# Fourteen kept steps in place of seven: an attention kernel that transposes more of its exponentials instead of computing them twice

## The chip, the cores and the metric

The kernel runs on one core of a Trainium2 chip. Its engines work side by side and meet through semaphores: TensorE (PE in the profile; its weight loads are PEld), VectorE (DVE), ScalarE (ACT), GpSimd (POOL) and SyncE (SP), which here only issues DMA transfers. The metric is device time in microseconds of one execution; the median of 3 runs of the kernel before is 692.13 us (692.12 to 693.17).

## What is computed

A conditioned self-attention with a residual: 8 batches, 512 positions, width 512, 16 heads of 32.

```python
Q = _split_heads(x @ Wq.T + bq)
K = _split_heads(x @ Wk.T + bk)
V = _split_heads(x @ Wv.T + bv)
tQ = _split_heads(tokens @ Wq.T + bq)      # tokens: one row per batch
tK = _split_heads(tokens @ Wk.T + bk)
cQ = Q + tQ
cK = K + tK
scores = jnp.einsum('bhqd,bhkd->bhqk', cQ, cK) / jnp.sqrt(jnp.float32(HEAD_DIM))
attn = jax.nn.softmax(scores, axis=-1)
out = jnp.einsum('bhqk,bhkd->bhqd', attn, V)
return x + out.transpose(0, 2, 1, 3).reshape(B, S, D_MODEL)
```

All arithmetic is in 32-bit floats.

## The kernel before

**Steps.** The work is cut into T = 32 steps: step t is batch t // 4 and a group of four heads, which fill the 128 partitions with 4 x 32 rows. For a step the kernel needs three things: the row maxima and row sums of the scores (queries on the partitions), the exponentials with the keys on the partitions, and those times V.

**Two kinds of step.** In a *plain* step the scores are computed twice. First row by row (`row_scores`, L585): VectorE takes the negated maxima (`one_max`, `row_max_of`, L552 and L594), ScalarE takes exponentials whose only use is their sum (`denominators`, L640). The maxima are split into three bf16 parts (`split_max`), turned by a DMA transpose (`turn_max`, L666), and in the next step `exponentials` computes the scores again with keys on the partitions (L695), subtracts the maxima through a small matmul with ones (L692), and ScalarE writes the exponentials `e` (L706). In a *blocked* step the row exponentials of L640 are kept instead, in a buffer `blocks` of 128 x 8192 values, and turned: VectorE transposes every 32 x 32 square in place (`turn_blocks`, L605, eight units of 128 x 1024, unit n belonging to query chunk n // 2), and DMA transfers exchange squares between the four groups of 32 partitions. Before, the exchange (`swap_blocks`, L624) is a swap through two `between` buffers: for each half of the queries three moves of six transfers of 32 rows x 4 KB, each move after the one before. Such a step has no second scores, no `e` and no `maxT`. Blocked are the steps 3, 7, ... 27. There is one `blocks` buffer (pool `eb`, `bufs=1`).

**Items.** The loop over t = 1 ... 28 has four items a step: V (the weighted sum of step t - 1, `weighted`, and its output), and q, k, v, which project for a later batch. In each item TensorE does, in order, the second scores of t (plain steps), the row scores of step t + 1, query chunk i + 1 (in the last item: t + 2, chunk 0), and a product or the V sum. The projections use seven half-size products in place of eight for a 2 x 2 split (`MADE_OF`, products 1 to 7 of `product`, L441): the item of an odd step does products 1, 6, 7 and half of 2 (`first_products`, or `first_by_others` in blocked steps, where ScalarE copies and GpSimd adds), that of an even step 4, 5, 3 and the other half of 2 (`other_products`, whose adds are VectorE's).

**What sets the order.** TensorE, VectorE, ScalarE and GpSimd run what they are given in the written order (`manual_schedule`), and so, all but a few transfers at the start, does SyncE. PSUM has eight banks; `begin` and `released` hand them from item to item, so that an item's scores go to the banks that were freed first. `turn_more` says after which item how many units are turned, `SWAPS` after which item which move is issued; loads of x blocks and residuals are issued in the last item of a step, outputs at once in `send`.

## Time and profile before

| | |
|---|---|
| median of 3 runs | 692.13 us |
| span of the profiled execution (the page gives no other time of it) | 687.9 us |
| PE busy | 677.3 us (98%) |
| DVE busy | 563.3 us (82%) |
| ACT busy | 563.7 us (82%) |
| POOL busy | 233.3 us (34%) |
| granted TensorE clock | 1.000 |
| transfers of the exchange (L624) | 252 of 128 KB, 2.4 us from issue to landing |

A line of a timeline reads: start in us from the span's start, duration, engine, line of the kernel, operation, output<-input, and how many stand in it; in brackets the idle time ahead of it and what ended it. A line of the chain of waits has start, duration and the work that the end of the run is followed back through. Groups have the number of instructions, their busy time, the mean in ns and the idle time ahead. `SPq` are the DMA issues of SyncE; their duration is the issue, not the transfer. Instructions of one engine overlap a little at their ends, so the distance between two starts is the better measure of what one costs. A waiting matmul often shows no idle time: its weights' load is what waits, so the distance between items is again the better measure.

### The profile page before, as it was taken

Reading aid. Unit: us, or ns where it says so; the run is one execution under the profiler, and the core shown is the slowest. Engines: PE = TensorE matmul, PEld = TensorE weight load, DVE = VectorE, ACT = ScalarE, POOL = GpSimd, SP = SyncE. Lnnn points to the kernel's source line nnn. Section 1 sums busy time; section 2 is a strip of 40 time slices with the busy share of each in tenths; the row PEclk is TensorE's granted clock in tenths of the full one; section 3 lists DMA queues with packets and bytes.
Section 4 is the critical chain, followed back from the end, with each engine's and each line's share of the span. In section 5 each row is a group of like instructions: output and inputs, shape, how many; then the busy total and the mean of one; then the engine's idle time right before and its main releaser. Section 6 shows DMA issues by size and latency. Waiting matters only on the chain.

```text
span 687.9 us, 22054 instructions
## 1 busy us (share of the span) xinstructions
PE 677.3 (98%) x8824; PEld 311.7 (45%) x8824; DVE 563.3 (82%) x878; ACT 563.7 (82%) x1427; POOL 233.3 (34%) x315
## 2 busy tenths in 40 slices
PE   9999999999999999999999999999999999999997
PEld 7444444444445444444444444453544544444332
DVE  4798799967989689886998778996798967987777
ACT  2589887988879898898888988798887989888664
POOL 3722412424233242424314252252423324241361
PEclk9999999999999999999999999999999999999999
DMA  6633235654376543663456624665427622376311
GB/s 183 104 54 60 40 64 133 129 106 70 52 155 143 90 71 78 132 155 61 68 118 122 143 49 77 135 125 113 72 40 154 148 54 41 66 135 151 53 31 31
DMA packets 231674, 65.50 MB, mean 95 GB/s; under 512 B 221834, under 2 KB 222346, under 8 KB 231572
## 3 DMA queue, kind: packets, MB, share of 16 engines
q1 hardware_dynamic: 229812, 63.05, 47.4%
q8 instruction: 69, 1.13, 0.7%
q10 hardware_dynamic: 1760, 1.05, 0.5%
q14 instruction: 33, 0.27, 0.1%
HBM read 19.75 MB, written 8.39 MB: 41 GB/s over the span
## 4 chain that ended last, share of the span: by engine, by line
PE 88%; DMA 3%; POOL 3%; SPq 2%; ACT 1%; DVE 1%; issue 1%; DVEq 0%; POOLq 0%; ACTq 0%
PE psum L441 37%; PE psum L715 16%; PE psum L585 16%; PE psum L695 11%; PE psum L692 4%; PE psum L384 2%; DMA maxT<-split 2%; SPq L784 1%; ACT psum L640 1%; SPq L188 1%; DMA xr<-in_x_dram 1%; POOL res L781 1%; DMA w_q<-in_L_cond_Wq_dram 1%; DVE nmax L552 1%; PE psum L725 1%
## 5 line engine op out<-in xcount | busy, mean ns | idle before, releaser
L640 ACT ACTIVATE psum<-psum,nmax 128x512 f32<-128x512 f32 x368 | 244.7, 673 | 29.0 <-DVE nmax L552 21.2
L552 DVE TENSOR_REDUCE nmax<-psum 128x1 f32<-128x512 f32 x298 | 191.3, 683 | 79.6 <-PE psum L585 77.2
L706 ACT ACTIVATE e<-psum 128x512 f32<-128x512 f32 x376 | 194.2, 602 | 61.2 <-PE psum L695 57.7
L585 PE MATMUL psum<-kT,qT 32*128 32x512 f32 x1024 | 143.0, 605 | 0.0
L594 DVE TENSOR_REDUCE nmax<-psum 128x2 f32<-128x1024 f32 x101 | 122.5, 1214 | 1.3 <-PE psum L585 1.3
L695 PE MATMUL psum<-qT,kT 32*128 32x512 f32 x752 | 96.7, 587 | 0.0
L715 PE MATMUL psum<-e,v 128*32 128x512 f32 x800 | 95.3, 597 | 0.0
L780 POOL TENSOR_TENSOR res<-res,recs 128x512 f32<-128x512 f32 x30 | 31.4, 1048 | 172.4 <-DVE res L779 172.4
L196 POOL TENSOR_TENSOR xr<-xr,bvs 128x512 f32<-128x512 f32 x30 | 38.4, 1280 | 141.8 <-DMA xr<-in_x_dram 141.8
L585 PEld LDWEIGHTS psum<-kT,qT 32*128 32x128 f32 x1024 | 60.9, 182 | 52.7 <-issue 22.0
L640 ACT ACTIVATION_READ_ACCUMULATOR psum<-psum,nmax 128x1 f32 x368 | 78.7, 214 | 0.0
L640 ACT ACTIVATE blocks<-psum,nmax 128x512 f32<-128x512 f32 x112 | 76.2, 719 | 0.0
L605 DVE STREAM_TRANSPOSE blocks<-blocks 128x1024 f32<-128x1024 f32 x56 | 68.5, 1223 | 0.0
L441 PE MATMUL psum<-wc_v,xc 128*32 128x256 f32 x768 | 50.2, 379 | 0.0
L441 PE MATMUL psum<-xc,wc_q 128*32 128x256 f32 x720 | 47.1, 379 | 0.0
L441 PE MATMUL psum<-xc,wc_k 128*32 128x256 f32 x720 | 47.1, 379 | 0.0
L715 PEld LDWEIGHTS psum<-e,v 128*32 128x32 f32 x800 | 20.8, 110 | 51.4 <-issue 29.2
L692 PE MATMUL psum<-maxT,onesb 3*128 3x512 bf16 x376 | 37.1, 385 | 3.0 <-DMA maxT<-split 2.3
L781 POOL TENSOR_TENSOR res<-res,xr 128x512 f32<-128x512 f32 x30 | 38.5, 1282 | 2.4
L695 PEld LDWEIGHTS psum<-qT,kT 32*128 32x128 f32 x752 | 37.4, 185 | 1.7
L441 PE MATMUL psum<-wT_v,xT 128*32 128x256 f32 x512 | 36.8, 382 | 0.0
L779 DVE STREAM_TRANSPOSE res<-psum 128x512 f32<-128x512 f32 x28 | 20.1, 717 | 18.4 <-PE psum L715 15.4
(179 smaller groups left out, 862.9 us busy)
## 6 DMA issues: line engine op xcount, KB each, us to landing
between<-blocks SPq DMA_DIRECT2D x84, 128.0 KB, 2.4
blocks<-blocks SPq DMA_DIRECT2D x84, 128.0 KB, 2.3
blocks<-between SPq DMA_DIRECT2D x84, 128.0 KB, 2.4
out_dram<-res SPq DMA_DIRECT2D x122, 64.0 KB, 1.9
xr<-in_x_dram SPq DMA_DIRECT2D x120, 64.0 KB, 2.4
x<-in_x_dram SPq DMA_DIRECT2D x112, 64.0 KB, 2.4
w_q<-in_L_cond_Wq_dram SPq DMA_DIRECT2D x4, 256.0 KB, 4.2
w_v<-in_L_cond_Wv_dram SPq DMA_DIRECT2D x16, 64.0 KB, 2.3
```

What stands on the lines that cost most here:

```text
L196: nc.gpsimd.tensor_tensor(xr[t], xr[t], bias, ALU.add)
L441: nc.tensor.matmul(pt[r], still[:, r], moving, start=(kc == kcs[0]), stop=(kc == kcs[-1]))
L552: nc.vector.tensor_reduce(nmax[t][:, qc, j : j + 1, 0], pt, AX.X, ALU.max, negate=True)
L585: nc.tensor.matmul(pt, qkT["q", t][r, qc * P : (qc + 1) * P], qkT["k", t][r, :], start=True, stop=True,)
L594: nc.vector.tensor_reduce(nmax[t][:, qc, pr * 2 : pr * 2 + 2, 0], pt, AX.X, ALU.max, negate=True)
L605: nc.vector.transpose(e, e)
L640: nc.scalar.activation(to, of, AF.Exp, bias=nmax[t][:, qc, j, :], accum_out=sums[t][:, qc, j, :],)
L692: nc.tensor.matmul(bank[j], onesb[r, :], maxT[t][r, :], start=True, stop=False)
L695: nc.tensor.matmul(bank[j], qkT["k", t][r, kc * P : (kc + 1) * P], qkT["q", t][r, :], start=False, stop=True,)
L706: nc.scalar.activation(e[:, i, :], bank[pr * 2 + i], AF.Exp)
L715: nc.tensor.matmul(pt[j * HD : (j + 1) * HD, :], vs[b % 2][:, kc, (g * HG + j) * HD : (g * HG + j + 1) * HD], e, start=(kc == chunks[0]), ...
L781: nc.gpsimd.tensor_tensor(y, y, xr.pop(t), ALU.add)
```

## The change

The odd steps 1, 3, ... 27 are blocked, 14 instead of 7, and

- the row exponentials of a blocked step go to an `arena` of 14 rooms of 128 x 1024 (`rows_kept`: rooms 0 to 3 for the first half of the queries, 4 to 7 for the second); the `e` of plain steps use rooms 8 to 13, 0 and 1 (`room_for_e`). The pool of ten `e` buffers is gone;
- the exchange comes first and the turn after it: `exchange` moves each half with 16 transfers of 32 rows x 4 KB from the arena into `blocks`, none of which waits for another; then VectorE turns the eight units in place, one after each of the items k and v of the even step ahead, one after V and q of the odd step, two after k and v;
- in odd steps the items do products 1, 6, 2, 7 whole (`four_products`: ScalarE's copies, GpSimd's adds), in even steps 5, 4, 3 (`three_products`: VectorE's adds);
- the V item is always first; SyncE's work is listed by item (`ORDERS`): even steps issue the first exchange after V, and store, residual and the second exchange after k; odd steps store after q, residual and x blocks after k. `send` only puts its output on a list that `store` empties;
- x blocks have two buffers instead of three, `q`/`k` pairs two instead of three, residuals one; the turned maxima go into the unused half of `wT_v`; the residual's bias is added on GpSimd at the head of `weighted`.

```diff
@@ -68,14 +68,15 @@
-    BLOCKED = [t for t in range(3, T - 4, G)]
+    ROOMS = 14
+    BLOCKED = list(range(1, T - 4, 2))
...
-    xp = ctx.enter_context(tc.tile_pool(name="xp", bufs=3))
+    xp = ctx.enter_context(tc.tile_pool(name="xp", bufs=2))
...
-    qkp = ctx.enter_context(tc.tile_pool(name="qkp", bufs=3))
-    ep = ctx.enter_context(tc.tile_pool(name="ep", bufs=10))
+    qkp = ctx.enter_context(tc.tile_pool(name="qkp", bufs=2))
+    ep = ctx.enter_context(tc.tile_pool(name="ep", bufs=1))
@@ -181,19 +182,40 @@
-                xr[t] = late[0][:, 2, :].rearrange("p (f e) -> p f e", e=BL)
+                xr[t] = late_part(t % 2 * 10 + 2).rearrange("p (f e) -> p f e", e=BL)
...
-                xr[t] = op.tile([P, NB, BL], F32, tag="xr", name=f"xr_{t}")
+                xr[t] = op.tile([P, NB, BL], F32, tag="xr", name=f"xr_{t}", bufs=1)
...
-            bias = bvs[:, g, :].unsqueeze(1).broadcast_to([P, NB, BL])
...
+    def add_bias(t):
+        if turned_by_vector(t):
+            bias = bvs[:, t % G, :].unsqueeze(1).broadcast_to([P, NB, BL])
+        else:
...
+    arena = ep.tile([P, ROOMS, NP * S], F32, tag="arena", name="arena")
+    place = [0]
+    def room_for_e(t, kc, pr):
+        if t + 1 in BLOCKED and kc == 0 and pr == 0:
+            place[0] = 8
+        i = place[0]
+        place[0] = (i + 1) % ROOMS
+        return arena[:, i, :].rearrange("p (i s) -> p i s", s=S)
+    def rows_kept(t, half):
+        a = arena[:, half * HG : (half + 1) * HG, :]
+        return a.rearrange("p g (c h s) -> p g c h s", c=2, h=HG)
@@ -486,29 +508,43 @@
-    def first_by_others(n, b, u, dens, small, at):
+    def four_products(n, b, u, dens, small, at):
...
+        m1 = c2[:, 0, :]
...
+        product(n, b, u, 2, two_[:, :HS])
...
+            nc.scalar.copy(c1, two_.rearrange("p (h s) -> p h s", h=2) if c1.shape[1] == 2 else two_)
...
+            i = "qk".index(n)
+            nc.scalar.activation(c1, halves(two_), AF.Identity, bias=tok[:, i, u * 2, b : b + 1])
+            nc.scalar.activation(c22, one_[:, HS:], AF.Identity, bias=apart_tok[:, i, u, b : b + 1])
+        nc.gpsimd.tensor_tensor(c1, c1, twice(m1), ALU.add)
...
+    def three_products(n, b, u, dens, small, at):
+        dens()
+        one_, two_ = banks(at[0]), banks(at[1])
+        product(n, b, u, 5, one_[:, HS:])
+        product(n, b, u, 4, one_[:, :HS])
+        small()
+        product(n, b, u, 3, two_[:, :HS])
+        c1, c12, c2, c22 = parts_of(n, b, u)
+        nc.vector.tensor_tensor(c12, one_[:, HS:], c12, ALU.add)
+        nc.vector.tensor_tensor(c2, halves(one_), twice(c22), ALU.add)
+        nc.vector.tensor_tensor(c12, two_[:, :HS], c12, ALU.add)
+        if n != "v":
+            for g in range(2):
+                qkT[n, b * G + u * 2 + g] = pair_of(b * G + u * 2, n)[:, g, :]
@@ -604,24 +640,15 @@
-    APART = [(a, g) for a in range(HG) for g in range(a + 1, HG)]
-    between = {}
-    def swap_blocks(t, half, move):
-        def part(a, g):
-            e = blocked[t][a * BL : (a + 1) * BL, g, half * 2 : half * 2 + 2]
-            return e.rearrange("p c h s -> p (c h s)")
-        if move == 0:
-            between[t, half] = [
-                ep.tile([P, 2, S], F32, tag="e", name=f"between_{t}_{half}_{i}") for i in range(2)
-            ]
-        for n, (a, g) in enumerate(APART):
-            at = (n + 2) % HG * BL
-            kept = between[t, half][n // HG][at : at + BL].rearrange("p i s -> p (i s)")
-            to, of = [(kept, part(a, g)), (part(a, g), part(g, a)), (part(g, a), kept)][move]
-            nc.sync.dma_start(to, of)
+    def exchange(t, half):
+        if t not in blocked:
+            blocked[t] = room(f"blocks_{t}")
+        for g in range(HG):
+            for a in range(HG):
+                of = arena[a * BL : (a + 1) * BL, half * HG + g, :]
+                to = blocked[t][g * BL : (g + 1) * BL, a, half * 2 : half * 2 + 2]
+                nc.sync.dma_start(to.rearrange("p c h s -> p (c h s)"), of)
@@ -629,9 +656,9 @@
-                if t not in blocked:
-                    blocked[t] = room(f"blocks_{t}")
-                to = blocked[t][:, :, qc, j, :].rearrange("p g (c e) -> p g c e", e=BL)
+                to = rows_kept(t, qc // 2)[:, :, qc % 2, j, :].rearrange(
+                    "p g (c e) -> p g c e", e=BL
+                )
@@ -658,11 +685,15 @@
+    def room_for_max(t):
+        return wT["v"][:, len(maxT) % 2, HS:].bitcast(BF16)
...
-        maxT[t] = op.tile([P, S], BF16, tag="maxT", name=f"maxT_{t}")
+        maxT[t] = room_for_max(t)
@@ -700,7 +731,7 @@
-            e = ep.tile([P, 2, S], F32, tag="e", name=f"e_{t}_{kc}_{pr}")
+            e = room_for_e(t, kc, pr)
@@ -762,8 +793,8 @@
+        if t:
+            add_bias(t)
@@ -775,13 +806,20 @@
-        y = op.tile([P, NB, BL], F32, tag="res", name=f"res_{t}")
+        y = op.tile([P, NB, BL], F32, tag="res", name=f"res_{t}", bufs=2)
...
-        b, g = divmod(t, G)
-        for h in range(HG):
-            nc.sync.dma_start(spread(out[b], g * P + h * BL), y[h * BL : (h + 1) * BL])
+        to_store.append((t, y))
+    to_store = []
+    def store():
+        while to_store:
+            t, y = to_store.pop(0)
+            b, g = divmod(t, G)
+            for h in range(HG):
+                nc.sync.dma_start(spread(out[b], g * P + h * BL), y[h * BL : (h + 1) * BL])
@@ -957,12 +997,14 @@
+    exchange(1, 0)
...
+    exchange(1, 1)
@@ -972,45 +1014,45 @@
+        hold()
...
-            hold()
-            other_products(n, b, r // 2, dens, small, (0, 3))
+            three_products(n, b, r // 2, dens, small, (0, 3))
...
-        elif blocks and n == "v":
-            first_products(n, b, r // 2, dens, small, 5, 4, hold)
-            released(6, 7, 0, 1, 2, 3, 5, 4)
...
-            hold()
-            first_by_others(n, b, r // 2, dens, small, 4)
+            four_products(n, b, r // 2, dens, small, 4)
...
-            first_products(n, b, r // 2, dens, small, 1, 0, hold)
+            four_products(n, b, r // 2, dens, small, 0)
...
-    TURNED = [((1, 1), (0, 1), (0, 1), (0, 1)), ((0, 0), (0, 1), (0, 1), (0, 1))]
-    turned = {}
-    def turn_more(t, i, late):
-        for u in (t, t + 1):
-            if u in BLOCKED:
+    TURNED = {(-1, 2): 1, (-1, 3): 1, (0, 0): 1, (0, 1): 1, (0, 2): 2, (0, 3): 2}
+    turned = {1: 2}
+    turn_blocks(1, range(2))
+    def turn_more(t, i):
+        for u in (t - 1, t, t + 1):
+            if u in BLOCKED and (t - u, i) in TURNED:
...
-                turned[u] = n + TURNED[t + 1 - u][i][late]
+                turned[u] = n + TURNED[t - u, i]
...
-    SWAPS = {
-        (-1, 2): [(0, 0)],
-        (-1, 3): [(0, 1), (0, 2)],
-        (0, 3): [(1, 0)],
-        (1, 0): [(1, 1)],
-        (1, 1): [(1, 2)],
+    ORDERS = {
+        (1, 0): [],
+        (1, 1): ["store"],
+        (1, 2): ["residual", "x"],
+        (1, 3): [],
+        (0, 0): [0],
+        (0, 1): [],
+        (0, 2): ["store", "residual", 1],
+        (0, 3): [],
...
-        items = ["q", "k", "v", "V"] if t - 1 in BLOCKED else ["V", "q", "k", "v"]
+        items = ["V", "q", "k", "v"]
@@ -1035,29 +1077,27 @@
-                    weighted(t - 1, banks(0), banks(1), lambda: turn_more(t, i, 0))
+                    weighted(t - 1, banks(0), banks(1), nothing)
...
-            if i == 0 and r == 0:
+            if i == 0 and r % 2 == 0:
...
-            if i == 2 and r == 1:
-                turn_x(t + NC + 3)
-                turn_x(t + NC + 4)
-            if i == 3:
-                load_blocks()
...
-            if i == 3:
-                load_residual(t + 1)
-            turn_more(t, i, 1)
-            for u in (t - 1, t, t + 1):
-                if u in BLOCKED and (t - u, i) in SWAPS:
-                    for swap in SWAPS[t - u, i]:
-                        swap_blocks(u, *swap)
+            turn_more(t, i)
+            for what in ORDERS[t % 2, i]:
+                if what == "store":
+                    store()
+                elif what == "residual":
+                    load_residual(t)
+                elif what == "x":
+                    load_blocks()
+                elif t + 1 in BLOCKED:
+                    exchange(t + 1, what)
```

More of the change, by code (lines that the diff above doesn't have):

```diff
@@ L341, in transpose_x @@
         leaves(xT[b][:, :, sc * P : (sc + 1) * P], pt.rearrange("p (c s) -> p c s", c=NC))
-        if n:
-            load_block(n + 3)
+        if n > 1:
+            load_block(n + 2)
     def turn_x(n):
@@ L351, in turn_x @@
         nc.vector.transpose(xT[b][:, cc, :], xs[n].rearrange("p f i -> p (f i)"))
-        to_load.append(n + 3)
+        to_load.append(n + 2)
     to_load = []
@@ L496, in first_by_others @@
         small()
-        product(n, b, u, 2, two_[:, :HS], (0,))
+        product(n, b, u, 2, two_[:, :HS])
         product(n, b, u, 7, one_[:, HS:])
-        m1 = c2[:, 0, :]
         nc.scalar.copy(m1, one_[:, :HS])
         if n == "v":
-            nc.scalar.copy(c1[:, 0, :], two_[:, :HS])
-            nc.scalar.copy(c12, two_[:, HS:])
+            nc.scalar.copy(c1, two_.rearrange("p (h s) -> p h s", h=2) if c1.shape[1] == 2 else two_)
             nc.scalar.copy(c22, one_[:, HS:])
         else:
-            nc.scalar.copy(c1, halves(two_))
-            add = tok[:, "qk".index(n), u * 2 + 1, b : b + 1]
-            nc.scalar.activation(c22, one_[:, HS:], AF.Identity, bias=add)
-        for o in (c1[:, 0, :], c12):
-            nc.gpsimd.tensor_tensor(o, o, m1, ALU.add)
-        nc.gpsimd.tensor_tensor(c22, c22, c12, ALU.add)
+            i = "qk".index(n)
+            nc.scalar.activation(c1, halves(two_), AF.Identity, bias=tok[:, i, u * 2, b : b + 1])
+            nc.scalar.activation(c22, one_[:, HS:], AF.Identity, bias=apart_tok[:, i, u, b : b + 1])
+        nc.gpsimd.tensor_tensor(c1, c1, twice(m1), ALU.add)
+        nc.gpsimd.tensor_tensor(c22, c22, c12, ALU.add)
+    def three_products(n, b, u, dens, small, at):
[12 more added lines that the diff above has]
+                qkT[n, b * G + u * 2 + g] = pair_of(b * G + u * 2, n)[:, g, :]
     def other_products(n, b, u, dens, small, at):
@@ L680, in transpose_max @@
             )
-        maxT[t] = op.tile([P, S], BF16, tag="maxT", name=f"maxT_{t}")
+        maxT[t] = room_for_max(t)
         copy(maxT[t], pt[:, :S])
@@ L793 @@
     tok = const.tile([P, 2, NC, B], F32, tag="tok", name="tok")
+    apart_tok = const.tile([P, 2, NC // 2, B], F32, tag="aparttok", name="aparttok")
     part = {}
@@ L818, in condition_end @@
         )
+        on.tensor_tensor(apart_tok[:, i], tok[:, i, 1::2], tok[:, i, 0::2], ALU.subtract)
     warm = one()
@@ L908 @@
     load_residual(0)
+    add_bias(0)
     advance()
@@ L951 @@
     load_blocks()
-    load_residual(1)
     turn_x(NC + 3)
@@ L1116, in crossed @@
         for pr in (1, 0):
-            e = ep.tile([P, 2, S], F32, tag="e", name=f"e_{t}_{kc}_{pr}")
+            e = room_for_e(t, kc, pr)
             es[t, kc, pr] = e
@@ L1128 @@
     t = T - 3
+    load_residual(t)
+    load_residual(t + 1)
     row(4)
@@ L1145 @@
     part_of(t, banks(2), [0, 1], lambda: transpose_max(t + 1, banks(3), nc.scalar.copy))
+    add_bias(t - 1)
     send_parts(t - 1, den)
+    store()
     t = T - 2
@@ L1151 @@
     apart = masked(t - 1)
-    load_residual(t)
     load_residual(t + 1)
+    for u in (t - 1, t, t + 1):
+        add_bias(u)
     part_of(t - 1, banks(2), [2, 3])
@@ L1162 @@
     send_parts(t - 1, den)
+    store()
     row(2)
@@ L1194 @@
     nc.vector.reciprocal(rec, den[:, :, 0:1])
-    y30 = op.tile([P, NB, BL], F32, tag="res", name=f"res_{t - 1}")
+    y30 = op.tile([P, NB, BL], F32, tag="res", name=f"res_{t - 1}", bufs=2)
     nc.vector.transpose(y30.rearrange("p f e -> p (f e)"), parts[t - 1])
```

## The prediction

> **What bounds the kernel now.** I read the page first, then the chain of waits over one blocked step, then the timelines of TensorE, VectorE, ScalarE and SyncE.

> ```profile
> span 687.9 us, 22054 instructions
> PE 677.3 (98%) x8824; PEld 311.7 (45%) x8824; DVE 563.3 (82%) x878; ACT 563.7 (82%) x1427; POOL 233.3 (34%) x315
> PE 88%; DMA 3%; POOL 3%; SPq 2%; ACT 1%; DVE 1%; issue 1%; DVEq 0%; POOLq 0%; ACTq 0%
> ```

> TensorE is the bound: 98% busy, 88% of the chain. The chain gives the length of the items of a blocked step and of a plain product item:

> ```profile
> 191.91 1.07 PE psum L585 x8
> 196.62 1.07 PE psum L585 x8
> 197.69 3.16 PE psum L441 x56
> 200.85 1.07 PE psum L585 x8
> 209.31 0.33 PE psum L692 x4
> 214.51 0.33 PE psum L692 x4
> ```

> In a blocked step the V item takes 196.62 - 191.91 = 4.71 us and a product item 200.85 - 196.62 = 4.23; a plain product item takes 214.51 - 209.31 = 5.20. The timeline of TensorE gives the plain V item, 394.76 - 389.08 = 5.68, and the loop's ends:

> ```profile
> 66.28 0.39 PE L692 MATMUL psum<-maxT,onesb 3*128 3x512 bf16 x4
> 389.08 0.40 PE L692 MATMUL psum<-maxT,onesb 3*128 3x512 bf16 x4
> 394.76 0.40 PE L692 MATMUL psum<-maxT,onesb 3*128 3x512 bf16 x4
> 640.11 0.39 PE L692 MATMUL psum<-maxT,onesb 3*128 3x512 bf16 x4
> ```

> Steps 1 to 28 run from 66.28 to 640.11: 573.8 us, or 40.99 for two steps. Pure TensorE work is 7 x (3 x (5.68 + 3 x 5.20) + 4.71 + 3 x 4.23) = 568.7, so only 5.1 us of the loop is waiting. Nothing but less TensorE work can make it faster, and any new wait shows at once.

> **TensorE's work.** Seven odd steps (1, 5, ... 25) become blocked. The split 3.5 + 3.5 of block products becomes 4 in odd and 3 in even steps: half a product is 8 of the 56 matmuls, 8/56 x 3.16 = 0.45 us. An even step then takes 5.68 + 3 x (5.20 - 0.45) = 19.93, an odd one 4.71 + 3 x (4.23 + 0.45) = 18.75, a pair 38.68, and 14 pairs 541.5. On TensorE alone the loop gains 573.8 - 541.5 = 32.3 us.

> **The way through the exchange.** A blocked step's exponentials can go to the blocks only when those of the block step before have left them: there is one such buffer. So in even step E (times from its first matmul) the first exchange waits for the V item (5.68) and for the row exponentials of that item. In the item that begins at 389.08 these end at 395.13:

> ```profile
> 394.93 0.20 ACT L640 ACTIVATION_READ_ACCUMULATOR psum<-psum,nmax 128x1 f32 x1
> ```

> That is 6.05 after the start; I take 6.15 for SyncE's first transfer. The same kind of transfer (32 rows of 4 KB) is in the trace, 18 in a row:

> ```profile
> 105.91 4.93 SPq L624 DMA_DIRECT2D between<-blocks  x6
> 114.71 4.97 SPq L624 DMA_DIRECT2D blocks<-between  x6
> 374.40 3.72 SPq L624 DMA_DIRECT2D between<-blocks  x6
> 378.22 4.65 SPq L624 DMA_DIRECT2D blocks<-blocks  x6
> 382.91 3.76 SPq L624 DMA_DIRECT2D blocks<-between  x6
> blocks<-between SPq DMA_DIRECT2D x84, 128.0 KB, 2.4
> ```

> 18 take 12.27 us at 374.40 (0.68 each) and 13.77 at 105.91 (0.765); a move without a long issue takes 3.72 (0.62). I take 0.70, near the ordinary stretch, and keep 0.63 and 0.765 as ends. Fifteen intervals are 10.5, landing 2.4: the exchange is through at E + 19.05 (18.0 to 20.0).

> VectorE's first turn of these blocks stands in its order behind the k products of item 2, ahead of the row maxima of item 3. In the item that begins at 389.08 the adds of the item before end at 389.96:

> ```profile
> 388.34 0.41 DVE L523 TENSOR_TENSOR v<-psum,v 128x256 f32<-128x256 f32 x1
> 389.27 0.69 DVE L463 TENSOR_TENSOR v<-psum,v 128x512 f32<-128x512 f32 x1
> ```

> That is 0.88 after the item; the new last add is half as wide (0.41 for 0.69), so VectorE gets there at 5.68 + 2 x 4.75 + 0.6 = E + 15.8 and **stands still until E + 19.05**. Behind it, in order:

> ```profile
> 427.84 1.23 DVE L605 STREAM_TRANSPOSE blocks<-blocks 128x1024 f32<-128x1024 f32 x1
> 429.12 1.29 DVE L552 TENSOR_REDUCE nmax<-psum 128x1 f32<-128x512 f32 x2
> 431.45 0.41 DVE L523 TENSOR_TENSOR kT<-psum,kT 128x256 f32<-128x256 f32 x1
> 356.87 1.25 DVE L552 TENSOR_REDUCE nmax<-psum 128x1 f32<-128x512 f32 x2
> 359.28 0.66 ACT L640 ACTIVATE psum<-psum,nmax 128x512 f32<-128x512 f32 x1 [0.28 <-DVE nmax L594]
> ```

> A turn takes 1.2 and the maxima begin at E + 20.25. ScalarE does the third of their four rows 359.28 - 356.87 = 2.41 later, in 0.66. The odd step's V item writes the bank of that third row, so its first matmul comes at 20.25 + 3.07 = E + 23.3 rather than 19.93 + 1.07 = E + 21.0. **TensorE stands still 2.3 us in each pair.** From there it runs 3.64 (V) and 3 x 4.68 to the next even step: 41.0 us from E, as against 40.99 before. The last two steps have no exchange, so there are 13 such waits: 541.5 + 13 x 2.3 = 571.4, a gain of 2.4.

> **What else is queued, and why it costs nothing or little** (X is the landing, E + 19.05).

> ```profile
> 420.57 0.24 DVE L760 RECIPROCAL recs<-psum 128x16 f32<-128x16 f32 x1
> 421.96 0.72 DVE L779 STREAM_TRANSPOSE res<-psum 128x512 f32<-128x512 f32 x1
> L640 ACT ACTIVATE psum<-psum,nmax 128x512 f32<-128x512 f32 x368 | 244.7, 673 | 29.0 <-DVE nmax L552 21.2 <-DVE nmax L594 6.6 <-ACT psum L640 0.4
> L706 ACT ACTIVATE e<-psum 128x512 f32<-128x512 f32 x376 | 194.2, 602 | 61.2 <-PE psum L695 57.7 <-issue 2.3 <-ACT e L706 1.2
> ```

> VectorE, from X to the next V item: eight turns (9.6), five items of maxima at 431.45 - 429.12 = 2.33 (11.65), one set of adds (0.93 + 0.41), one output (0.24 + 0.72): 23.5 us, and that V item wants the last turn at X + 24.0. Slack 0.5. The added 56 turns (56 x 1.2 = 67 us) take the place of the first products' copies and adds, which go to ScalarE and GpSimd. ScalarE in an even product item: four of 244.7 / 368 and four of 194.2 / 376 make 4.73 of 4.75; what that adds falls into the 2.3 us in which TensorE waits anyway. The four-product items are:

> ```profile
> 364.56 0.37 ACT L500 COPY qT<-psum 128x256 f32<-128x256 f32 x1
> 365.29 0.50 ACT L508 ACTIVATE qT<-psum,tok 128x256 f32<-128x256 f32 x1
> 365.50 1.42 POOL L510 TENSOR_TENSOR qT<-qT 128x256 f32<-128x256 f32 x2 [2.49 <-ACT qT L506]
> ```

> ScalarE's copies, 364.56 to 365.79, take 1.2 an item, beside four row exponentials of 0.66 in 4.68: hidden; by the same counting the last copy frees its bank some 0.25 us before the next row scores want it. GpSimd's adds get no longer by more than their width, and it is 34% busy.

> SyncE issues in a pair 32 transfers at 0.70, 8 each of stores, residuals and x blocks, and one transpose:

> ```profile
> 368.93 1.22 SPq L666 DMA_TRANSPOSE maxT<-split  x1
> 414.87 4.25 SPq L170 DMA_DIRECT2D x<-in_x_dram  x8
> 425.20 1.96 SPq L784 DMA_DIRECT2D out_dram<-res  x4
> 427.20 2.92 SPq L188 DMA_DIRECT2D xr<-in_x_dram  x4
> ```

> At 0.53 (4.25 / 8) to 0.61 (4.88 / 8) the small ones take 24 x 0.55 = 13.2: 22.4 + 13.2 + 1.2 = 36.8 of 41.0 us, so the order matters. First exchange to X - 1.7, store and residual to X + 2.7, second exchange landing at X + 15.6, wanted by VectorE behind the k maxima of the odd step at X + 16.2; store behind it; transpose of the maxima issued at X + 18, landing 2.5 later, wanted at X + 22; residual and x blocks to X + 26; the next first exchange may start at X + 28. Slacks 0.6, 1.5 and 2. For what these thin slacks (0.25 to 0.6) let through I add 0.1 us a pair, 1.3 in all, and keep 0 and 1.0 a pair as ends.

> The two-deep x buffers and the single residual buffer cost nothing as long as the loads are through at X + 26 + 2.4 = X + 28.4, since their readers come behind the V item that ends at X + 27.6, and TensorE's bank waits have 2.3 us of room in the even step. The shared rooms 0 and 1, which the last exponentials of an even step reuse, have been read by the first eight transfers at about E + 14, before E + 17.

> **The start.** The exchange for step 1 begins behind the row exponentials that end at 51.44; in the built program's order two x blocks stand among it:

> ```profile
> 51.18 0.26 ACT L640 ACTIVATION_READ_ACCUMULATOR psum<-psum,nmax 128x1 f32 x1
> 66.47 0.69 DVE L463 TENSOR_TENSOR v<-psum,v 128x512 f32<-128x512 f32 x1
> ```

> 51.4 + 4.3 + 10.5 + 2.4 = 68.6, while VectorE is free at 67.2 and then turns two pieces (2.4) ahead of step 1's maxima, which start at 71.0 in place of 67.4; after the room that the banks give, TensorE loses some 1.8 us (0 if the landing comes by 65; 3.6 if all of the lag shows). The end keeps its work: 0.

> **Sum.** -32.3 + 29.9 + 1.3 + 1.8 = +0.7 us: a span of 688.6. The page gives the span alone; the median of the runs is 692.13, 4.2 above it, which I add: **692.8, say 693 us**. That is the before time, to within 0.2%, which is about what a measurement of this kernel can tell from no change. The ends of the transfer (0.63: waits of 1.25 us; 0.765: 3.3) move it by -14 and +13: 679 to 706 for this case.

> [...]

> **Rivals.**
> *The exchange is hidden (faster).* If sixteen transfers landed by E + 16.7 (X less the 2.3 of the wait), no pair would wait: 692.1 - 32.3 + 1.8 = 661.6 us. It needs 0.55 us a transfer, which the small transfers have (0.53) and no move in the trace has (0.62 at best). For it speaks that six-transfer moves also carried waits for each other. Chance 0.14.
> *The second exchange is late (slower).* SyncE is at 90% of a pair. Two long issues in one exchange (each adds 0.9 to 1.2, as in 4.93 against 3.72), or a store that waits for GpSimd, eat the slack of 0.6; from there VectorE's chain to the next V item grows by what is over, in both exchanges. At 1.0 us a pair beyond the main case: 693 + 13 = 706 us. Against it: the second exchange has a spare 2 us ahead of the next one, and delays do not pile up. Chance 0.28.

> **How the numbers follow.** Main case 0.58, of it 0.20 faster, 0.12 same and 0.26 slower than 692.1, since its unknowns (thin slacks) lean to more waiting. With the rivals: faster 0.34, same 0.12, slower 0.54. The range 677 to 708 takes in the ends of the transfer and the second rival and leaves out the first and the far tail, some 0.2.

> **What would show it.** Right: TensorE busy falls by about 30 us while the span stays; ahead of each V item of steps 3 to 27 a gap or stretched row-score group of about 2.3 us, put down to ScalarE's exponentials or VectorE's maxima; VectorE idle about 3 us ahead of the first turn of a block, released by the blocks' transfers; pairs of 41.0 us. Wrong: turns without idle time ahead of them and pairs near 38.7 (first rival), or idle time ahead of the fifth turn and pairs over 42 (second).

## The result, and the profile after

The changed kernel takes 710.65 us (median of four runs, 707.54 to 717.27) against 692.12 us before: a ratio of 1.0279, 95% interval 1.0226 to 1.0333. It is slower, and slower than the forecast's range. Of all executions that follow, one is left out of its kernel's ratio, though not of its median, being over 1.5% slower than the fastest of that kernel: 711.18 us at clock 0.987, with the first turn behind item 3.

The page of the changed kernel, its first lines, the chain by engine and by line, and the clock by slices:

```profile
span 710.6 us, 21535 instructions
PE 691.2 (97%) x8488; PEld 305.1 (43%) x8488; DVE 571.3 (80%) x810; ACT 544.6 (77%) x1399; POOL 280.3 (39%) x330
PEclk9999999999999999999999999999899999999999
PE 67%; SPq 16%; DMA 5%; DVE 4%; ACT 3%; issue 3%; POOL 0%; DVEq 0%; ACTq 0%; POOLq 0%
```

TensorE has 336 matmuls fewer, and yet its busy time is up from 677.3 to 691.2 us: a matmul whose operands or clock are late counts as busy (eight row-score matmuls held by a wait show 2.88 us for 1.03, eight of the V sum at half clock 1.94 for 1.06; both are below). Of the chain it holds 67% in place of 88%; SyncE's issuing (16%) and transfers (5%) have come into it. The clock line has an 8 where before it had none.

One pair of steps in which the clock stays full, from the timelines of TensorE, SyncE and VectorE (E = 301.25 is the start of the even step, 342.45 that of the next):

```profile
301.25 0.39 PE L723 MATMUL psum<-wT_v,onesb 3*128 3x512 bf16 x4
307.52 10.86 SPq L651 DMA_DIRECT2D blocks<-arena  x16
320.36 1.25 DVE L641 STREAM_TRANSPOSE blocks<-blocks 128x1024 f32<-128x1024 f32 x1 [2.41 <-DMA blocks<-arena]
322.01 2.88 PE L621 MATMUL psum<-kT,qT 32*128 32x512 f32 x8
342.45 0.39 PE L723 MATMUL psum<-wT_v,onesb 3*128 3x512 bf16 x4
```

The exchange begins at E + 6.27, VectorE stands still 2.41 us ahead of its first turn, which starts at E + 19.11, and the odd V item's row scores, 1.03 us where nothing waits, are stretched to 2.88. The pair takes 41.20 us. That is the forecast's mechanism in the forecast's place. Over all 13 pairs the first turn starts at E + 19.5 in the mean.

In another pair TensorE's timeline has the V item of the odd step, after such a wait:

```profile
195.77 1.13 PE L621 MATMUL psum<-kT,qT 32*128 32x512 f32 x4
197.33 1.82 PE L621 MATMUL psum<-kT,qT 32*128 32x512 f32 x4 [0.43 <-ACT psum L667]
199.08 1.94 PE L746 MATMUL psum<-arena,v 128*32 128x512 f32 x8
200.91 3.47 PE L746 MATMUL psum<-arena,v 128*32 128x512 f32 x24
```

The same 8 and 24 matmuls take 1.06 and 2.76 us elsewhere (324.83 and 325.77). The view by stretches, with the granted clock behind the engines' busy times, shows why. Its rows are stretches at half clock, with one (195.55) of the 3.41 us ahead of such a stretch:

```profile
core 0: us, PE busy (x) PEld busy (x) DVE busy (x) ACT busy (x) POOL busy (x), PEclk, DMA share, GB/s
76.08:79.49 3.41, 3.41 (x40) 1.74 (x36) 3.41 (x5) 2.28 (x7) 3.33 (x4) 0.50 0.90 207
113.63:117.04 3.41, 3.41 (x26) 0.75 (x28) 3.41 (x6) 1.87 (x7) 1.28 (x1) 0.50 0.92 209
195.55:198.96 3.41, 2.98 (x16) 0.88 (x8) 3.41 (x6) 2.24 (x7) 0.00 (x0) 1.00 0.61 99
198.96:202.37 3.41, 3.41 (x25) 0.90 (x28) 3.41 (x6) 1.88 (x5) 1.28 (x1) 0.50 0.89 211
...
410.59:414.00 3.41, 3.41 (x28) 1.15 (x28) 3.28 (x5) 1.71 (x5) 1.16 (x1) 0.50 0.91 208
...
495.92:502.75 6.83, 6.74 (x38) 1.80 (x42) 5.10 (x9) 4.38 (x13) 1.28 (x1) 0.50 0.89 204
```

One more, of 3.41 us, begins at 366.21; ahead of the kernel's last microseconds there are no others. All stand behind a wait of TensorE; before the change the clock was full from 5.3 to 688 us. In the loop five of the 13 pairs hold such a stretch, 20.5 us together; these five take 43.2 to 45.9 us, the other eight 41.0 to 42.2, 41.47 in the mean. From VectorE's first turn to the next even step the five take 24.2 us in the mean and the eight 22.1. The spread between runs goes with it as well: spans of 705.1, 706.8, 710.6 and 715.5 us had mean clocks of 0.989, 0.988, 0.981 and 0.977.

### The profile page after: what moved, and what is told of

Read it like the earlier page. It is cut to its first block, busy times and chain, and to the rows that moved or that the text cites. A ratio compares the mean times of both kernels' runs of the same rounds, so it can differ in the third digit from the quotient of the medians.

```text
span 710.6 us, 21535 instructions
## 1 busy us (share of the span) xinstructions
PE 691.2 (97%) x8488; PEld 305.1 (43%) x8488; DVE 571.3 (80%) x810; ACT 544.6 (77%) x1399; POOL 280.3 (39%) x330
## 4 chain that ended last, share of the span: by engine, by line
PE 67%; SPq 16%; DMA 5%; DVE 4%; ACT 3%; issue 3%; POOL 0%; DVEq 0%; ACTq 0%; POOLq 0%
PE psum L463 27%; SPq L651 16%; PE psum L746 15%; PE psum L621 15%; PE psum L726 4%; DMA out_dram<-res 2%; PE psum L406 2%; ACT psum L667 2%; PE psum L723 2%; DVE nmax L588 2%; DMA blocks<-arena 1%; DVE blocks L641 1%; DVE nmax L630 1%; ACT arena L667 1%; DMA early<-in_x_dram 1%
## 5 line engine op out<-in xcount | busy, mean ns | idle before, releaser
L667 ACT ACTIVATE psum<-psum,nmax 128x512 f32<-128x512 f32 x256 | 169.0, 662 | 91.1 <-DVE nmax L588 79.8
L621 PE MATMUL psum<-kT,qT 32*128 32x512 f32 x1024 | 177.1, 625 | 10.9 <-ACT psum L667 10.9
L641 DVE STREAM_TRANSPOSE blocks<-blocks 128x1024 f32<-128x1024 f32 x112 | 134.5, 1221 | 40.0 <-DMA out_dram<-res 24.8
L737 ACT ACTIVATE arena<-psum 128x512 f32<-128x512 f32 x264 | 136.4, 602 | 33.7 <-PE psum L726 24.5
L667 ACT ACTIVATE arena<-psum,nmax 128x512 f32<-128x512 f32 x224 | 152.8, 697 | 5.3 <-issue 4.9
L746 PE MATMUL psum<-arena,v 128*32 128x512 f32 x576 | 77.8, 659 | 0.0
L726 PE MATMUL psum<-qT,kT 32*128 32x512 f32 x528 | 67.9, 587 | 0.0
L746 PE MATMUL psum<-blocks,v 128*32 128x512 f32 x448 | 51.9, 596 | 0.0
L667 ACT ACTIVATION_READ_ACCUMULATOR psum<-psum,nmax 128x1 f32 x256 | 51.8, 202 | 0.0
L463 PE MATMUL psum<-wc_v,xc 128*32 128x256 f32 x768 | 50.6, 381 | 0.0
L463 PE MATMUL psum<-xc,wc_q 128*32 128x256 f32 x720 | 48.3, 387 | 0.0
L667 ACT ACTIVATION_READ_ACCUMULATOR arena<-psum,nmax 128x1 f32 x224 | 47.8, 213 | 0.0
L463 PE MATMUL psum<-xc,wc_k 128*32 128x256 f32 x720 | 47.4, 381 | 0.0
L810 DVE STREAM_TRANSPOSE res<-psum 128x512 f32<-128x512 f32 x28 | 19.5, 697 | 30.0 <-PE psum L746 30.0
L463 PE MATMUL psum<-wT_v,xT 128*32 128x256 f32 x512 | 34.3, 382 | 0.2 <-ACT arena L737 0.2
L746 PEld LDWEIGHTS psum<-arena,v 128*32 128x32 f32 x576 | 15.9, 118 | 42.8 <-issue 23.5
## 6 DMA issues: line engine op xcount, KB each, us to landing
blocks<-arena SPq DMA_DIRECT2D x448, 128.0 KB, 2.4
```

The lines of the kernel that those rows point to most:

```text
L463: nc.tensor.matmul(pt[r], still[:, r], moving, start=(kc == kcs[0]), stop=(kc == kcs[-1]))
L621: nc.tensor.matmul(pt, qkT["q", t][r, qc * P : (qc + 1) * P], qkT["k", t][r, :], start=True, stop=True,)
L641: nc.vector.transpose(e, e)
L667: nc.scalar.activation(to, of, AF.Exp, bias=nmax[t][:, qc, j, :], accum_out=sums[t][:, qc, j, :],)
L726: nc.tensor.matmul(bank[j], qkT["k", t][r, kc * P : (kc + 1) * P], qkT["q", t][r, :], start=False, stop=True,)
L737: nc.scalar.activation(e[:, i, :], bank[pr * 2 + i], AF.Exp)
```

## The experiments

The theory to be tested: the pair is set by the wait at VectorE's first turn, as forecast, and on top of it the waits let TensorE's clock drop. The rivals: the second exchange is late (the forecast's own rival), VectorE has no room, or the clock drops for another reason. Four figures are given for each run: median, ratio to the kernel before with its interval, and, both of the one execution that was profiled, the granted clock and the mean of the 13 pairs between the starts of steps 2 and 28 (42.43 us in the changed kernel: from 89.93 to 641.58). `...` marks what is left out of a piece of code.

**Fill the wait.** 30 matmuls of 128 columns that nobody reads, ahead of each block step's V item:

```diff
             begin(w)
...
+            if blocks and i == 0:
+                for _ in range(30):
+                    nc.tensor.matmul(banks(0)[:, :P], onesb, onesb, start=True, stop=True)
```

> The changed kernel with 30 extra matmuls of 128 columns ahead of each blocked step's V item, written to a bank that is free there, so that TensorE works through most of the wait of 2 to 3 us. Theory A (the waits let the clock drop): granted clock 1.000, no stretch at half clock, pairs of steps near 41.2 us, about 698 us instead of 710.65. Rival B (the drops do not come from idle time, or the extra time over the forecast is SyncE's): clock still about 0.98, time 709 or more, the filling being extra work.

Measured: 707.65 us, 1.0231 (1.0205 to 1.0258), clock 0.997, pairs of 42.14 us. With half of the filling:

> The kernel with filled waits, with 16 instead of 30 extra matmuls, about 1.0 instead of 1.85 us of each wait. Theory A (short rests of a wait do not let the clock drop, and the filling itself is free): clock 0.995 or more and 705 to 708 us, as with 30. Rival B (the filling lengthened the pairs): 700 to 704 us. Rival C (what is left of the wait is enough to let the clock drop): clock 0.98 to 0.99 and 708 us or more.

Measured: 707.0 us, 1.0221 (1.0187 to 1.0254), clock 0.997, pairs of 41.73 us. TensorE's timeline with 30:

```profile
407.76 1.85 PE L1063 MATMUL psum<-onesb 128*128 128x128 bf16 x30
409.54 1.30 PE L621 MATMUL psum<-kT,qT 32*128 32x512 f32 x8
410.78 1.06 PE L746 MATMUL psum<-arena,v 128*32 128x512 f32 x8
```

The filling lies where the wait was; 0.27 us of it is left. In the profiled executions the stretches at half clock are gone but for one in the loop with 30 and none with 16, so the drops do come from the waits. (With 16 the profiled execution is the fastest, 703.56 us; the other three had clocks of 0.993 to 0.995 and took 706.12 to 709.10, so half of the filling does not always keep the clock full.) But theory A's 698 us did not come, not even in the execution with 30 whose clock was 1.000 (706.99 us). The pairs without a stretch take 41.89 us here. The filling stands in the wait's place and does not shorten the way through the exchange: the first turn starts at E + 19.7 in these pairs, and 22.2 us follow it. Theory A's 41.2 us is the length of the one pair shown above, in which VectorE waits 2.41 us; the mean is 2.85. The V items in the even step end up to 0.7 us late here, and the exchange starts with them; what the filling adds beyond that stays open.

**Move the turn.** The first turn, whose wait holds the maxima of item 3, goes behind item 3, or one turn goes on into the odd step:

```diff
-    TURNED = {(-1, 2): 1, (-1, 3): 1, (0, 0): 1, (0, 1): 1, (0, 2): 2, (0, 3): 2}
+    TURNED = {(-1, 3): 2, (0, 0): 1, (0, 1): 1, (0, 2): 2, (0, 3): 2}   # one
+    TURNED = {(-1, 3): 1, (0, 0): 2, (0, 1): 1, (0, 2): 2, (0, 3): 2}   # the other
...
```

> The changed kernel with the first turn of each block taken from behind item 2 of the even step to behind item 3, where two turns now stand together. Theory A (VectorE, held at its first turn, holds the row maxima of item 3 and through them TensorE): VectorE no longer idle ahead of that turn, the wait of TensorE ahead of the odd V item falls from 2.3 us to about 0.6, pairs near 39.4 us, clock near 1.00, 672 to 678 us. Rival B (the exchange is late for what comes after it as well, or VectorE has no room for two turns there): the wait only moves into the odd step, pairs of 41 us or more, 695 to 711 us.

> The changed kernel with the first turn of each block left out behind item 2 of the even step and done as a second one behind the V item of the odd step. Theory A (what holds TensorE is VectorE standing still ahead of the maxima of item 3): the wait ahead of the odd V item falls as with the turn put behind item 3, VectorE has 2.4 us of turns in the odd V item instead of 1.2, pairs of 39.4 to 40.2 us, 672 to 688 us. Rival B (VectorE's work from the landing to the next V item is what sets the pair): as slow as the changed kernel, 695 to 711 us.

Measured: 696.44 us, 1.0071 (1.0046 to 1.0095), clock 1.000, pairs of 41.24 us; and 700.03 us, 1.0111 (1.0077 to 1.0145), clock 0.999, pairs of 41.13 us. In the profiled executions the wait ahead of the odd V item is gone and with it the drops of the clock, which are most of these 10 to 14 us; the pair is little shorter than the changed kernel's pairs at full clock (41.47). That is rival B in both. (The second kernel's profiled execution is its fastest, 694.65 us; four of its six took 700.0 to 701.4 us at clocks of 0.994 to 0.998.) SyncE's timeline, and VectorE's and TensorE's at the next even step, with the turn behind item 3:

```profile
506.73 10.92 SPq L651 DMA_DIRECT2D blocks<-arena  x16
517.75 2.21 SPq L822 DMA_DIRECT2D out_dram<-res  x4
520.01 2.10 SPq L189 DMA_DIRECT2D xr<-in_x_dram  x4
522.21 11.55 SPq L651 DMA_DIRECT2D blocks<-arena  x16
```

```profile
535.74 2.37 DVE L641 STREAM_TRANSPOSE blocks<-blocks 128x1024 f32<-128x1024 f32 x2 [0.85 <-DMA out_dram<-res]
541.72 2.04 PE L621 MATMUL psum<-kT,qT 32*128 32x512 f32 x8
```

The second exchange, behind store and residual, is issued to 533.76, and the last four turns begin two microseconds later; they now hold the even V item (its row scores take 2.04 for 1.03). The next first exchange waits for that V item. The bracket names the store, which was issued at 535.01, 0.73 us before; no store whose landing is known lands in less than 1.7 us (1.7 to 4.1 in the changed kernel, 2.1 in the median), so it is the exchange, issued just ahead of it, that ended this wait. So a second loop of about 41 us lies under the first, hidden by an equal one.

**Divide the exchange over two queues.**

```diff
-                nc.sync.dma_start(to.rearrange("p c h s -> p (c h s)"), of)
+                queue = nc.sync if a % 2 or t == 1 else nc.gpsimd
+                queue.dma_start(to.rearrange("p c h s -> p (c h s)"), of)
```

> The changed kernel with every second transfer of each exchange issued by GpSimd instead of SyncE (from step 3 on). Theory A (the 10.4 us of an exchange are SyncE's issuing, 0.64 us apiece): the two halves run side by side, the last landing comes at about E + 15 instead of E + 19, VectorE does not stand still, pairs of 39 to 39.5 us, 670 to 678 us, unless GpSimd's own work is held up by its issuing. Rival B (the engines that move the data are the limit): the landing stays at E + 18 or later, pairs of 41 us or more, 695 to 711 us.

Measured: 704.97 us, 1.0202 (1.0178 to 1.0225), clock 0.989, pairs of 41.53 us. SyncE's share is issued in 5.38 us in the pair below, where the changed kernel's whole exchange took 10.86, but the first turn still starts at E + 19.1 in the mean (19.5 in the changed kernel): rival B's side. Two causes are in the trace, and no run separates them. GpSimd, which finishes a multiplication and an addition of the output first, issues its eight from 222.49 in this pair, 3.2 us after SyncE's first:

```profile
219.30 5.38 SPq L652 DMA_DIRECT2D blocks<-arena  x8
222.49 3.94 POOL L652 DMA_DIRECT2D blocks<-arena  x8
```

and the engines that move the data are all but full while both issue (last two columns: share busy, GB/s):

```profile
222.50:226.50 4.00, 4.00 (x52) 1.92 (x48) 2.91 (x6) 3.99 (x11) 3.98 (x10) 1.00 0.91 245
226.50:231.00 4.50, 4.50 (x68) 2.17 (x60) 3.23 (x6) 4.11 (x12) 3.54 (x5) 1.00 0.95 234
```

**Break the second loop.** SyncE's store of the even step goes behind the second exchange, alone and together with the later first turn; in a third kernel the even step's residual goes to GpSimd as well, and from item k to right behind the first exchange:

```diff
-        (0, 2): ["store", "residual", 1],
-        (0, 3): [],
+        (0, 2): ["residual", 1],
+        (0, 3): ["store"],
```

> The changed kernel with SyncE's store of the even step moved from ahead of the second exchange to behind it (item 3); the turns are as in the changed kernel. Theory A (two loops of about 41 us lie over each other: one from the first exchange over VectorE's first turn and the row maxima of item 3, one from the first exchange over store, residual and second exchange to the last turns and the V item): only the second gets shorter, by 2.2 us; the wait at the first turn stays, pairs 41 us, clock still below 0.995, 700 to 710 us. Rival B (the second exchange alone sets the pair): pairs of 39 to 39.5 us, about 680 us.

> Both edits: the first turn put behind item 3, and SyncE's store of the even step behind the second exchange. Theory A (two loops, each shortened by its own edit): pairs of 39.3 to 40.2 us, clock 1.00, 672 to 684 us, faster than the kernel before. Rival B (VectorE is full, 9.6 us of turns with everything else between landing and V item): pairs stay at 41 us, 692 to 697 us.

> As the kernel with both edits, and the even step's residual issued by GpSimd, so that nothing stands between the two exchanges on SyncE. Theory A: the second exchange starts as soon as its row exponentials are there, 2 us earlier still; pairs of 38.9 to 39.5 us, 668 to 676 us, if GpSimd's issuing costs no more than the 0.5 us apiece that it took for the exchange. Rival B (VectorE is full): 41 us, 692 to 697 us. Rival C (GpSimd's issuing of short rows holds up its adds): later than the kernel with both edits.

Measured: the order alone 706.21 us, 1.0203 (1.0153 to 1.0254), clock 0.988, pairs of 41.93 us (41.22 in the ten without a stretch); with the later turn 685.19 us, 0.9899 (0.9875 to 0.9923), clock 0.996, pairs of 40.41 us; with the residual on GpSimd 683.08 us, 0.9882 (0.9865 to 0.9899), clock 0.998, pairs of 40.23 us. Either edit alone leaves the pairs at 41.2 us where the clock is full; both together bring them to 40.4: two loops of equal length. VectorE is not full, since the pairs fell. Both forecasts were too low, for the kernel with both edits by about 1 us, for the third by 7: there the second exchange starts at E + 17.4 in place of 20.1, as meant, but it no longer sets the pair. The group of VectorE's turns says the same, idle time ahead of all 112 of them in the changed kernel and in the third of these:

```profile
L641 DVE STREAM_TRANSPOSE blocks<-blocks 128x1024 f32<-128x1024 f32 x112 | 134.5, 1221 | 40.0 <-DMA out_dram<-res 24.8
```

```profile
L641 DVE STREAM_TRANSPOSE blocks<-blocks 128x1024 f32<-128x1024 f32 x112 | 133.1, 1217 | 2.8 <-DMA blocks<-arena 2.8
```

Where the first line names the store (`out_dram<-res`, 24.8 us of the 40.0), that store had been issued 0.2 to 1.1 us before the turn, too late to have landed; and with the order alone, where the store stands elsewhere, the wait at the first turn stays (2.6 us in the mean of the 13 pairs, 2.85 in the changed kernel). It is the exchange's last landing. In the third kernel's 13 pairs a turn waits for it once, 0.36 us; the rest of the 2.8 us is step 1's. Most pairs now take the same 40.15 us (531.16 - 491.01). This is not the 38.68 of pure TensorE work. What is left is read from TensorE's timeline in that pair:

```profile
491.01 0.39 PE L723 MATMUL psum<-wT_v,onesb 3*128 3x512 bf16 x4
492.10 1.42 PE L621 MATMUL psum<-kT,qT 32*128 32x512 f32 x8
502.95 1.36 PE L621 MATMUL psum<-kT,qT 32*128 32x512 f32 x8
511.74 1.15 PE L621 MATMUL psum<-kT,qT 32*128 32x512 f32 x8
516.45 1.85 PE L621 MATMUL psum<-kT,qT 32*128 32x512 f32 x8
531.16 0.39 PE L723 MATMUL psum<-wT_v,onesb 3*128 3x512 bf16 x4
```

Row scores (1.03 or 1.14 where nothing waits) are stretched by 0.4 in the even V item, 0.3 in its k item and 0.7 in the odd q item. The last follows two turns that stand together ahead of the maxima.

**Spread the turns.** From that kernel, one of those two goes behind the odd q item:

```diff
-    TURNED = {(-1, 3): 2, (0, 0): 1, (0, 1): 1, (0, 2): 2, (0, 3): 2}
+    TURNED = {(-1, 3): 1, (0, 0): 1, (0, 1): 2, (0, 2): 2, (0, 3): 2}
...
```

> The fastest kernel so far with one turn less behind item 3 of the even step and one more behind the q item of the odd step (1, 1, 2, 2, 2 in place of 2, 1, 1, 2, 2). Theory (the 40.14 us of a pair hold 0.7 us in which the q item's row scores wait for banks behind the two turns, and 0.4 us in which the even V item waits for the last two): the first goes, the second stays or grows by 0.2: pairs of 39.5 to 39.9 us, 675 to 680 us. Rival (VectorE, now with three items of 4.86 us in the odd step against 4.67 of TensorE, is late at the even V item): pairs of 40.2 to 41 us, 683 to 692 us.

Measured: 677.17 us, 0.9769 (0.9752 to 0.9785), clock 0.998, pairs of 39.95 us. Faster than both kernels. In this pair, as in ten others, the odd step now takes TensorE's work and no more:

```profile
508.13 1.15 PE L621 MATMUL psum<-kT,qT 32*128 32x512 f32 x8
526.82 0.40 PE L723 MATMUL psum<-wT_v,onesb 3*128 3x512 bf16 x4
```

18.69 us, against 18.75 in the forecast. The even step keeps the rest, 21.0 us for 19.93.

**Put the wait back.** In the 683 us kernel, whose waits are below 0.8 us, VectorE repeats a row maximum of item 3 and so holds the odd V item:

```diff
+            if i == 3 and t + 1 in BLOCKED:
+                for _ in range(2):        # 4 in the second kernel
+                    one_max(*rows, 0, banks(w))
             dens = lambda: denominators(*rows, w)
```

> The fastest kernel so far (first turn behind item 3, nothing between the exchanges; 683 us, waits of TensorE below 0.8 us, clock 0.998) with a wait put in on purpose: in each even step before a block step, VectorE takes the first row maximum of item 3 twice more, which holds ScalarE's row exponentials, and through them TensorE ahead of the odd V item, by about 1.3 us. Theory A (the clock drops where TensorE waits for about 2 us or more): 683 + 13 x 1.3 = 700 us, up to 705, clock 0.99 or more. Rival B (any wait does it): clock 0.98, 710 us or more. Rival C (the drops have nothing to do with the waits): clock 0.996 or more, about 700 us.

> The same with four more maxima in place of two: a wait of about 2.6 us ahead of each odd V item. Theory A: 683 + 13 x 2.6 = 717 us from the waits alone, with several stretches at half clock of 3.41 us, clock 0.985 or less, and 5 us or more on top: 722 to 735 us. Rival C (the drops have nothing to do with the waits): clock 0.996 or more and 714 to 719 us.

Measured: 723.64 us, 1.0437 (1.0408 to 1.0465), clock 0.976, pairs of 43.17 us; and 759.03 us, 1.0951 (1.0932 to 1.0971), clock 0.953, pairs of 45.97 us. Pair by pair, with two maxima and then with four (starts of even steps):

```profile
521.82 0.40 PE L723 MATMUL psum<-wT_v,onesb 3*128 3x512 bf16 x4
565.63 0.40 PE L723 MATMUL psum<-wT_v,onesb 3*128 3x512 bf16 x4
607.77 0.40 PE L723 MATMUL psum<-wT_v,onesb 3*128 3x512 bf16 x4
...
546.88:550.29 3.41, 3.41 (x32) 0.89 (x28) 2.83 (x5) 2.15 (x7) 0.00 (x0) 0.50 0.85 195
```

```profile
390.55 1.80 PE L621 MATMUL psum<-kT,qT 32*128 32x512 f32 x8 [3.43 <-ACT psum L667]
392.28 1.94 PE L746 MATMUL psum<-arena,v 128*32 128x512 f32 x8
```

With two, the wait came out at 1.9 us, not 1.3: five pairs take 42.05 us in the mean (the second above, 42.14), and eight, each with 3.41 us at half clock, take 43.88 (the first above, 43.81). One stretch so costs 1.8 us, about half its length. 683 + 13 x 1.9 + 8 x 1.8 + 1.7 for one at the start is 724. With four, the wait is 3.4 us or more and every pair has a stretch, six of the 13 one of 6.83. Rival C is out. Of theory A and rival B the figures fit B for the smaller dose, but both doses were larger than meant (3.4 us for 2.6 with four, so that theory A's 722 to 735 us was passed as well): waits of 0.8 us and less gave no drop in 13 pairs, waits of 1.9 us gave eight, of 3.4 us thirteen.

**The forecast's wait alone.** The store behind the second exchange and the wait filled, with the first turn where the change has it:

> The changed kernel with the store moved behind the second exchange and the waits ahead of the block steps' V items filled with 30 extra matmuls; the first turn stands where the change put it. What is left is the forecast's own wait alone, without the second exchange's lateness and without stretches at half clock. Theory A (the forecast missed these two and nothing else in the loop): clock 0.996 or more, pairs of 41.0 to 41.3 us, 13 x 1.0 = 13 us above the kernel with 40.14 us a pair (683), so 695 to 699 us. Rival B (the filling itself lengthens the pairs, or the wait at the first turn was undersized): pairs of 41.6 us or more, 703 us or more.

Measured: 707.52 us, 1.0186 (1.0163 to 1.0210), clock 0.997, pairs of 42.07 us: rival B. With full clock and the second loop broken, the wait at the first turn was longer than forecast. The first turn starts at E + 19.8 in the mean of the 13 pairs; the last transfer is issued 2.4 to 4.2 us ahead of it. From the first turn on, a pair without a stretch takes 22.1 to 22.3 us in the mean in all kernels whose first turn stands there (22.3 here), so that 19.8 + 22.3 = 42.1 is what the pairs have to take. Whether the filling itself delays the landing (19.3 with the order alone, 19.5 in the changed kernel) or the chip of that run does (the kernel before took 694.3 us on it) stays open.

## Why the prediction was wrong

**TensorE's work: right, but not reachable.** The odd step's 18.75 us was met (18.69) once nothing held it. The even step's 19.93 was not met: it takes 20.7 us in the mean in the 683 us kernel and 21.2 in the 677 us kernel, so 0.8 to 1.2 us of short waits stay in it. "What that adds falls into the 2.3 us in which TensorE waits anyway" was right: in the changed kernel's undisturbed pair the odd V item begins at E + 20.76 instead of 19.93, and its wait is 1.85 instead of 2.3.

**The way through the exchange: right in kind, short by half a microsecond.** Start at E + 6.2 (6.15 forecast) and pace of 10.4 us for fifteen intervals (10.5) were right. The landing of 2.4 us, a median over single transfers, was too little for the last of sixteen: the first turn follows the last issue by 2.9 us in the mean. So it starts at E + 19.5 and not 19.05, and the pair without a drop of the clock should take 19.51 + 22.1 = 41.6 us, not 40.98: 13 x 0.63, less the 1.3 us that the forecast had set aside for thin slacks, is 6.9 us.

**The step that failed: "TensorE stands still 2.3 us in each pair".** The forecast priced a wait at its own length. The measured price is that and the half clock behind it. The pairs are 42.43 us in the mean against those 41.6: 13 x 0.82 = 10.7 us, and half of the 20.5 us at half clock is 10.2; from the first turn on, the five pairs with a stretch take 24.2 us for 22.1, which also makes some 10 us. With the stretch at 76.08 (1.7 us, an estimate: half of its length), the clock took some 12.4 of the 22 us by which the span is longer than forecast (710.6 against 688.6). This is the account of one execution; the 1.8 us a stretch in the kernel with two maxima bear it out. The filled kernels do not give that much back: their ratios are 0.5 to 0.6% lower, 3 to 4 us, as their pairs are longer for a cause left open above.

**The start and the end.** Step 2 began at 89.93 instead of 86.8: 1.7 us of this is put down to the stretch at half clock, and 1.4 to a longer first wait (step 1's first turn began at 69.8 where the forecast had the landing at 68.6). From the start of step 28 to the end of the span it took 69.0 us, 1.3 more than forecast. So 12.4 + 6.9 + 1.4 + 1.3 make the 22.0 us. The run added 1.8 us to its span and not the 4.2 of before, which gives 2.4 back.

**The rivals.** "The exchange is hidden" did not come, and would not have given 661.6 us: with the exchange out of the way the best run is 677. "The second exchange is late" did not come as it was put, as a wait on top of the first: in the 13 pairs of the changed kernel a later turn waits once, 0.38 us. What came is a second bound of nearly the same length beside the first wait, which cost little by itself and took away most of what could be won by removing the first. "What is late next" had been asked of each slack; it had not been asked of the loop as a whole, from V item over both exchanges to the next V item. The slack of 0.6 us that the working gave the second exchange's landing said as much: a way with so little slack is a second bound, not a reserve.

## What to carry to other kernels

Price a wait of the bounding engine not by its length alone: look at whether it costs that engine its clock (here waits of 0.8 us and less did in none of 13 pairs, of 1.9 us in eight, of 3.4 us in all), and add what each stretch costs (here 1.8 us, about half of its 3.41). When a new wait appears, draw every loop that closes through it and compare their lengths: two loops of equal length hide each other, and an edit that shortens one shows nothing until the other is cut as well (here 41.2 us a pair at full clock with either edit, 40.4 with both). For the landing of a batch take the last transfer's, not the median of one (here 2.9 us from the last issue to the first turn, for 2.4).

## What the runs showed of the hardware

The data engines are not yet full while one exchange issues in the changed kernel (share and GB/s last), but nearly so in the 683 us kernel, where the second exchange follows the first at once:

```profile
307.52:318.38 10.86, 10.86 (x152) 5.48 (x152) 9.27 (x15) 9.52 (x24) 5.11 (x5) 1.00 0.74 171
```

```profile
502.00:507.00 5.00, 5.00 (x72) 2.53 (x72) 3.90 (x7) 4.99 (x13) 1.69 (x4) 1.00 0.95 210
509.00:513.00 4.00, 4.00 (x64) 1.93 (x64) 3.89 (x7) 4.00 (x11) 0.00 (x0) 1.00 0.96 206
```

That is 74% busy at 171 GB/s, and 95 to 96% at 206 to 210 GB/s, with one queue issuing; with two it was 91 to 95% at 234 to 245 GB/s, so that the busy share alone does not say how much more can be moved. The second queue took SyncE's issuing of an exchange from 10.86 us to 5.38 and 6.44 in one pair, and the rate rose; the first turn came only 0.4 us earlier. What a second queue would win that starts without GpSimd's 3.2 us of delay, no run shows.
